# Values of the self attention in tiles of 128 tokens across batches, for the last three of four groups

## The chip, the cores and the metric

The kernel runs on one core of one Trainium2 chip. The metric is the device time of one execution in microseconds: the median of three runs, and beside it one execution that the hardware profiler recorded. An engine's name stands for its queue of instructions: TensorE (PE) for matrix products, VectorE (DVE), ScalarE (ACT) and GpSimd (POOL) for elementwise work, SyncE (SP) for issuing most of the DMAs. Each works through its queue in order.

## The reference, cut to what matters

One decoder layer on 16 batches of 100 tokens with 512 features: causal self attention with 16 heads of 32, cross attention to 361 context tokens per batch, a mixture of 8 experts, each followed by a residual sum and a norm. The change lies in the self attention:

```python
q = (x @ w_q.T).reshape(b, s, NH, HD).transpose(0, 2, 1, 3)
k = (x @ w_k.T).reshape(b, s, NH, HD).transpose(0, 2, 1, 3)
v = (x @ w_v.T).reshape(b, s, NH, HD).transpose(0, 2, 1, 3)
score = jnp.einsum('bhqd,bhkd->bhqk', q, k) * scale
...
attn = jax.nn.softmax(score, axis=-1)
o = jnp.einsum('bhqk,bhkd->bhqd', attn, v)
return o.transpose(0, 2, 1, 3).reshape(b, s, H) @ w_o.T
```

The values `v` are computed for each token by itself; batches meet nowhere in them. The output is float32.

## The kernel before, in words

**Splitting.** A float32 product is made of three products of reduced-precision float32 parts (`mm3`, L143): high by high, high by low, low by high, on lines L145, L146, L147. A contraction over 512 features has four chunks of 128, so one product of a tile (`mmk`) is 12 matmuls. `split` (L133) makes the parts: a cast for the high part (L137 on ACT, or L139), a subtraction for the low part (L140, on DVE or POOL).

**The first stage** (self attention, the first 207 us of the span) treats the batches in four groups of four (`GB` = 4, `GT` = 400 tokens). Each group has four units, one for each 128 features, that is four heads. In unit (g, c) the kernel computes:

- `self_q` and `self_k`: features by tokens, with the 400 tokens of the group as the moving operand (names pq, pk);
- `self_v` (L301): for each batch, tokens by features. The batch's 100 tokens are the stationary operand, so the result's partitions are tokens, and the 512 features move. The result (pv) is copied by ACT (L309) to a tile `v` of 100 partitions;
- `self_scores` (L326): products of queries and keys for each head and batch; `self_softmax` (L352) works on DVE, POOL and ACT;
- `self_turn` (L388): transposes the probabilities on PE (pt), copied by ACT to pT (L395);
- `self_attend` (L397): for each batch r and head, `V[g, r]` is the stationary operand, with tokens as the contraction, so the 100 tokens of a batch have to lie in partitions 0 to 99 of a tile of their own. The result is stored to DRAM (o1d, L416).

**Order.** The loop at L548 goes over the 16 units; `at(u, j, ...)` hangs further work ahead of turn j of unit u: the next unit's queries and keys, the fetch and split of the next group's tokens (`fetch_x`, `split_x`), the next group's values, and the rows of weights for the next stage (`fetch_row`, `split_row`; stored in slots of two large arrays WH and WL; they pass through a pool `stage` with three buffers). The compiler's scheduler then orders each engine's instructions within the dependences, by its own model, so the list of `at` is not the final order.

**The handover to the next stage** begins inside the first one. The output projection works on tiles of 128 tokens across batches: `b_fetch(t)` (L428) loads tile t of the attention output from DRAM (ol) and the residual (xr), `b_split` casts it (olp), `b_out` (L445) multiplies by the output weights (pa), adds and normalizes (L451, then `layernorm`), and stores (L453); `b_xT` (L455) transposes the result (ptx). Tiles 0 to 4 are projected before the last unit ends. `b_open` (L424) closes the pool `a_x`, which holds the incoming tokens xf, and opens a pool in its place for ol, xr and olp; `ol` has two buffers, `xr` four. The numbers in the list at L530 are 4 u + j: the first fetch hangs on 44, that is unit 11, turn 0.

After the first stage come the queries of the cross attention (`b_q`, pq at L600), the cross attention, the experts, and a last stage in which tile after tile is projected (pp), summed, multiplied by the norm's weight (L1529) and normalized (L1589, L1594, L1618), with square roots on ACT (L1653, q_f) and their refinement on DVE (L1654 to L1668).

Of the kernel before, what the change touches and what calls it, by code (L numbers as in the profile page):

```python
# [9 lines left out]
FP = mybir.dt.float32  # L10
# [7 lines left out]
B, S, D = 16, 100, 512  # L18
T = B * S
KC = D // 128  # L20
# [8 lines left out]
GB = 4  # L29
NG = B // GB  # L30
GT = GB * S
TT = [(t, min(128, T - t)) for t in range(0, T, 128)]
EPS_LN = 1e-5
EPS_RMS = 1e-6
# [28 lines left out]
def tile_decoder_layer(  # L63
    ctx: ExitStack,
    tc: tile.TileContext,
    x: bass.AP,
    xT: bass.AP,
    ctxT: bass.AP,
    mask: bass.AP,
    wqT: bass.AP,  # L70
# [21 lines left out]
    nc = tc.nc  # L92
# [3 lines left out]
    def pool(stack, name, bufs=1, **k):  # L96
        return stack.enter_context(
            tc.tile_pool(name=name, bufs=bufs, reuse_waits="tile", **k)
        )
# [6 lines left out]
    def bank(tag, shape, name):  # L106
        return ps[-1].tile(shape, FP, name=name, tag=tag)
# [12 lines left out]
    def in_turn(ins, prev):  # L120

        if prev is not None:
            tc.add_manual_dep(
                ins.ins,
                prev.ins.name,
                mybir.DependencyInfo(
                    mybir.DependencyClass.NoSync, mybir.DependencyReason.DATA
                ),
                reason="in_turn",
            )  # L130
        return ins

    def split(dst, src, high=None, low=None):  # L133

        high, low = high or nc.scalar, low or nc.vector
        if high is nc.scalar:
            ins = nc.scalar.copy(dst.h, src)  # L137
        else:
            ins = high.tensor_copy(dst.h, src)  # L139
        low.tensor_tensor(dst.l, src, dst.h.bitcast(FP), ALU.subtract)  # L140
        return ins

    def mm3(out, a, b, start, stop):  # L143

        nc.tensor.matmul(out, a.h, b.h, start=start, stop=False)  # L145
        nc.tensor.matmul(out, a.h, b.l, start=False, stop=False)  # L146
        nc.tensor.matmul(out, a.l, b.h, start=False, stop=stop)  # L147

    def mmk(out, a, b, n=KC):
        for k in range(n):  # L150
            mm3(out, a(k), b(k), k == 0, k == n - 1)
# [38 lines left out]
    stage = pool(ctx, "stage", 3)  # L190
# [5 lines left out]
    def slot_of(s):  # L196
        return Pair(WH[:, s], WL[:, s])
# [8 lines left out]
    units = {}  # L206
# [7 lines left out]

    NT = len(TT)
    o1d = [dram.tile([128, KC, GT], FP, name=f"o1d_{g}") for g in range(NG)]
    x1d = [dram.tile([128, D], FP, name=f"x1d_{t}") for t in range(NT)]
# [4 lines left out]
    a_l, a_r = ExitStack(), ExitStack()  # L222
    xp = pool(a_r, "a_x", 1, side="right")
    w1 = pool(a_l, "a_1", 1)
    w2 = pool(a_l, "a_2", 2)
    w3 = pool(a_l, "a_3", 8)
    ps.append(pool(a_l, "ps_a", 2, space=PSUM))
    ps_s = pool(a_l, "ps_s", 1, space=PSUM)

    xg, V, Q, K, O, P = {}, {}, {}, {}, {}, {}  # L230

    def fetch_x(g):
        xg[g] = xp.tile([128, KC, GT], FP, name=f"xf_{g}", tag="xf")
        nc.sync.dma_start(xg[g], xT[g])

    def x_pair(g):

        s = 6 + g % 2
        return Pair(WH[:, s, :, :GT], WL[:, s, :, :GT])

# [7 lines left out]
    XF = {}  # L248
    xf = xp.tile([128, KC, GT], FP, name="xf_0", tag="xf")
    xg[0] = x_pair(0)  # L250
# [46 lines left out]
    def split_chunk(c):  # L297
        split(*chunk("q", c), nc.scalar, nc.gpsimd)
        split(*chunk("k", c), nc.scalar, nc.gpsimd)

    def self_v(g, r):  # L301
        pv = bank("mm" if g else "t", [S, D], f"pv_{g}_{r}")
        mmk(
            pv,
            lambda k: xg[g][:, k, r * S : (r + 1) * S],
            lambda k: units["wv_s"][:, k, :],
        )
        V[g, r] = w1.tile([S, D], FP, name=f"v_{g}_{r}", tag="v", bufs=8)
        nc.scalar.copy(V[g, r], pv)  # L309

    def self_q(g, c):
        cc = slice(c * 128, (c + 1) * 128)
        pq = bank("mm", [128, GT], f"pq_{g}_{c}")
        mmk(pq, lambda k: units["wq_s"][:, k, cc], lambda k: xg[g][:, k, :])

        Q[g, c] = w2.tile([128, GT], FP, name=f"qT_{g}_{c}", tag="qT")
        nc.scalar.activation(Q[g, c], pq, AF.Copy, scale=-1.0 / math.sqrt(HD1))
# [79 lines left out]
    def self_attend(g, c):  # L397

        av = bank("t", [128, GB, S], f"av_{g}_{c}")
        prev = None  # L400

        for r in range(GB):
            for j in (3, 0, 1, 2):
                h = c * 128 + 32 * j
                ins = nc.tensor.matmul(
                    av[32 * j : 32 * j + 32, r, :],
                    V[g, r][:, h : h + 32],
                    PT[g, c, j][:, r, :],
                    start=True,
                    stop=True,  # L410
                    tile_position=(0, 32 * j),
                )
                prev = in_turn(ins, prev)
        o = w2.tile([128, GT], FP, name=f"o_{g}_{c}", tag="o")
        nc.scalar.copy(o, av.rearrange("p r s -> p (r s)"))
        nc.sync.dma_start(o1d[g][:, c], o)  # L416
# [11 lines left out]
    def b_fetch(t):  # L428
        t0, n = TT[t]
        OL[t] = ol = inp["b"].tile([128, KC, 128], FP, name=f"ol_{t}", tag="ol")  # L430
        a = t0
        while a < t0 + n:
            g, o = divmod(a, GT)
            m = min(GT - o, t0 + n - a)
            nc.sync.dma_start(ol[:, :, a - t0 : a - t0 + m], o1d[g][:, :, o : o + m])
            a += m
        XR[t] = inp["b"].tile([128, D], FP, name=f"xr_{t}", tag="xr", bufs=4)
        nc.sync.dma_start(XR[t][:n], x_flat[t0 : t0 + n, :])

    def b_split(t):  # L440
        n = TT[t][1]
        ol = OL[t]
        OL[t] = pair(inp["b"], [128, KC, 128], f"olp_{t}", tag="olp")
        return split(OL[t][:, :, :n], ol[:, :, :n], low=nc.gpsimd)

    def b_out(t):
        t0, n = TT[t]
        o, xr = OL.pop(t), XR[t]
        pa = bank("mm", [128, D], f"pa_{t}")
        mmk(pa[:n], lambda k: o[:, k, :n], lambda k: units["wo_s"][:, k, :])  # L450
        nc.vector.tensor_tensor(xr[:n], pa[:n], xr[:n], ALU.add)  # L451
        layernorm(xr[:n], xr[:n], n, f"ln1_{t}")
        nc.sync.dma_start(x1d[t][:n], xr[:n])  # L453

    def b_xT(t):  # L455
        t0, n = TT[t]
        x1 = XR.pop(t)
        pt = bank("t", [128, KC, 128], f"ptx_{t}")
        for k in range(KC):
            nc.tensor.transpose(  # L460
                pt[:, k, :n], x1[:n, k * 128 : (k + 1) * 128], ident[:n, :n]
            )
        X1T[t] = slot_of(0)[:, t % KC].rearrange("p (k n) -> p k n", n=128)
        split(X1T[t][:, :, :n], pt[:, :, :n])
# [3 lines left out]
    def at(u, j, f, *a):  # L468
        extra.setdefault((u, j), []).append(lambda: f(*a))
# [24 lines left out]
    for u, (g, c) in enumerate(heads4):  # L494
        if u + 2 < NU:
            if u < 2:
                at(u, 0, split_chunk, u + 2)
            at(u, 0, self_k, *heads4[u + 2])
            at(u, 2, self_q, *heads4[u + 2])
        if g + 1 < NG:  # L500
            if c == 0:
                at(u, 1, fetch_x, g + 1)
                for k in range(2):
                    at(u, 3, split_x, g + 1, k)
            if c == 1:
                for k in range(2):
                    at(u, 1, split_x, g + 1, 2 + k)
            if c > 1:
                for r in range(2):
                    at(u, 1 + 2 * r, self_v, g + 1, 2 * (c - 2) + r)  # L510

    rows = [("wo_s", 3, kp(woT), k) for k in range(KC)]
    rows += [("wq_0", 4, Wqg[0], k) for k in range(KC)]
# [8 lines left out]
    for k in range(KC):  # L522
        i = 4 * NU - 8 + k
# [2 lines left out]
        at(i // 4, i % 4, behind, split_row, "wq_3", k)  # L526

    AHEAD = 5
    at(10, 0, b_open)
    for t, i in enumerate((44, 48, 52, 54, 58)):  # L530
        at(i // 4, i % 4, b_fetch, t)
        i += 2 if t == AHEAD - 1 else 4
        at(i // 4, i % 4, behind, b_split, t)
    for t, i in enumerate((51, 55, 59, 61, 62)):
        at(i // 4, i % 4, b_out, t)
    for t, i in enumerate((57, 60, 63)):
        at(i // 4, i % 4, b_xT, t)
# [1 line left out]
    self_q(0, 0)  # L539
    self_k(0, 0)  # L540
    self_scores(*heads4[0])
    self_v(0, 0)
    split_chunk(1)
    for r in range(1, GB):
        self_v(0, r)
    self_q(0, 1)
    self_k(0, 1)
    for u, unit in enumerate(heads4):  # L548
# [15 lines left out]
    w1 = pool(b_l, "b_1", 1)  # L564
# [27 lines left out]
    def b_q(t):  # L592
        t0, n = TT[t]
        x1T = X1T.pop(t)
# [83 lines left out]
    w1 = pool(c_l, "c_1", 1, side="right")  # L678
# [183 lines left out]
    for i, (b, g) in enumerate(order):  # L862
# [34 lines left out]
        if i % 3 == 2 and 8 <= i < 8 + 3 * NKV * KC:  # L897
            w, k = divmod((i - 8) // 3, KC)
# [12 lines left out]
    w1 = pool(d_l, "d_1", 1, side="right")  # L911
# [416 lines left out]
    for i in range(HEAD * NKV, len(parts)):  # L1328
        t, g = parts[i]
# [477 lines left out]
```

## Time and profile before

| what | value |
|---|---|
| median of three runs | 1411.22 us (1411.13 to 1414.11) |
| the profiled execution, its own time | 1423.84 us |
| span of that execution | 1422.1 us |
| mean granted clock of PE in it | 0.973 |
| matmuls and their weight loads | 7952 each |
| DVE, ACT, POOL busy | 66%, 53%, 50% of the span |
| matmuls for values (pv) in the first stage | 192, in 16 products |
| copies of values, ACT L309 | 16, median 587 ns |
| weights rows fetched by SP in the first stage | 20 (4 for f_wo_s, 16 for f_wq) |

The span is what the profiler recorded between the first and the last instruction of one execution. That execution's own time is 0.9% above the median of the plain runs; its parts are used for differences. "Busy" of PE overstates: matmuls are pipelined, and each one's recorded duration overlaps the next one's. What a matmul costs in a row of matmuls is the distance between two starts. A weight load (PEld) stands in its own row.

### The profile page before, as it was taken

To read this page: it belongs to the slowest core of one execution; us is meant where nothing else is said; L and a number is where in the kernel's file an instruction comes from. 1 tells how busy PE (TensorE), PEld (TensorE's weight loads), DVE (VectorE), ACT (ScalarE), POOL (GpSimd) and SP (SyncE) were. 2 spreads that over 40 slices of the span, in tenths; PEclk is the share of its full clock that TensorE was granted. 3 is DMA by queue.
4 is the path that set the end of the run, shared out by engine and by line. 5 is a ranking of instruction groups with operands and counts; after the bars stand their busy time and mean duration, and the time that the engine had idled before them with its cause. 6 is when DMAs were issued, how large, how long until landed. Compare 5 with 4: busy or idle time off the path is not lost.

```text
span 1422.1 us, 25158 instructions
## 1 busy us (share of the span) xinstructions
PE 1338.8 (94%) x7952; PEld 1109.5 (78%) x7952; DVE 939.8 (66%) x2960; ACT 756.9 (53%) x1899; POOL 708.8 (50%) x837
## 2 busy tenths in 40 slices
PE   8999989999999999999999999999999897899895
PEld 6888868888878887888888788878887675677773
DVE  5776577776467777767777667767653658654577
ACT  4666653444445666666565666656563233233356
POOL 6877663344245555555555545545454345431530
PEclk9999989999999999999999999999999999799997
DMA  5221254545442222233233213232536555667773
GB/s 158 72 93 51 73 158 115 130 91 111 101 93 77 53 60 69 70 77 76 69 70 82 70 43 70 70 70 54 132 84 198 170 167 164 189 207 232 247 254 125
DMA packets 197872, 159.79 MB, mean 112 GB/s; under 512 B 133322, under 2 KB 152878, under 8 KB 197742
## 3 DMA queue, kind: packets, MB, share of 16 engines
q1 hardware_dynamic: 187904, 137.83, 36.3%
q0 software_dynamic: 4576, 14.95, 3.5%
q10 hardware_dynamic: 5262, 5.41, 1.3%
q8 instruction: 65, 1.06, 0.3%
q14 instruction: 65, 0.53, 0.1%
HBM read 107.16 MB, written 50.99 MB: 111 GB/s over the span
## 4 chain that ended last, share of the span: by engine, by line
PE 69%; DVE 13%; DMA 8%; ACT 4%; issue 3%; POOL 1%; SPq 1%; ACTq 0%; DVEq 0%; POOLq 0%
PE pq L145 4%; PE pq L147 4%; PE pq L146 4%; PE pv L145 4%; PE pv L146 4%; PE pv L147 4%; PE ptp L767 3%; PE pk L145 3%; PE pk L147 3%; PE pk L146 3%; PE s L145 3%; PE s L147 3%; PE s L146 3%; PE av L146 2%; PE av L145 2%
## 5 line engine op out<-in xcount | busy, mean ns | idle before, releaser
L759 POOL TENSOR_SCALAR p<-p,sums 100x361 f32<-100x361 f32 x256 | 146.5, 577 | 100.2 <-DVE sums L758 89.2
L746 DVE CUSTOM_DVE_ANT_0 p<-s,nmask 100x361 f32<-100x361 f32 x256 | 132.9, 527 | 64.4 <-PE s L147 56.0
L757 ACT ACTIVATE p<-p,nm 100x361 f32<-100x361 f32 x256 | 153.2, 601 | 40.1 <-DVE nm L746 37.0
L140 DVE TENSOR_TENSOR pT_l<-ptp,pT_h 128x400 fp32r<-128x400 f32 (+1 forms) x192 | 107.4, 567 | 57.3 <-ACT pT_h L137 56.7
L145 PE MATMUL pq<-WH 128*128 128x512 f32 (+2 forms) x272 | 107.2, 394 | 5.7 <-DVE WH L139 5.7
L767 PE MATMUL ptp<-ident,p 100*128 100x100 f32 (+1 forms) x768 | 107.5, 252 | 0.0
L137 ACT CAST pT_h<-ptp 128x400 fp32r<-128x400 f32 (+1 forms) x192 | 91.2, 486 | 29.6 <-PE ptp L767 29.1
L767 PEld LDWEIGHTS ptp<-ident,p 100*128 100x128 f32 (+1 forms) x768 | 95.6, 152 | 13.4 <-POOL p L759 2.3
L140 POOL TENSOR_TENSOR cT_l<-cf,cT_h 128x512 fp32r<-128x512 f32 (+1 forms) x48 | 54.3, 1133 | 101.9 <-ACT cT_h L137 100.0
L146 PE MATMUL pq<-WL,WH 128*128 128x512 f32 (+2 forms) x272 | 104.6, 385 | 0.0
L147 PE MATMUL pq<-WH,WL 128*128 128x512 f32 (+2 forms) x272 | 104.5, 384 | 0.0
L147 PE MATMUL acc<-WH,ot_l 128*128 128x512 f32 (+1 forms) x208 | 85.9, 414 | 7.4 <-DVE ot_l L140 5.6
L145 PE MATMUL acc<-WH,ot_h 128*128 128x512 f32 (+1 forms) x208 | 85.8, 413 | 4.9 <-ACT ot_h L137 4.9
L145 PE MATMUL s<-kT_h,WH 128*100 128x362 f32 x256 | 88.2, 355 | 1.7 <-ACT kT_h L137 1.7
L145 PE MATMUL av<-pT_h,WH 128*128 128x400 f32 (+1 forms) x192 | 77.3, 402 | 11.5 <-ACT pT_h L137 11.2
L147 PE MATMUL s<-kT_h,WL 128*100 128x362 f32 x256 | 84.5, 330 | 0.0
L146 PE MATMUL acc<-WL,ot_h 128*128 128x512 f32 (+1 forms) x208 | 84.3, 405 | 0.0
L146 PE MATMUL s<-kT_l,WH 128*100 128x362 f32 x256 | 83.9, 328 | 0.0
L614 POOL TENSOR_TENSOR qs<-qs,r_q 128x512 f32<-128x512 f32 (+1 forms) x52 | 54.0, 1068 | 59.3 <-DVE r_q L169 48.9
L140 POOL TENSOR_TENSOR WL<-qf,WH 128x400 fp32r<-128x400 f32 x64 | 67.3, 1052 | 30.1 <-ACT WH L137 26.7
L145 PE MATMUL pv<-WH,cT_h 128*128 128x512 f32 (+1 forms) x192 | 79.6, 414 | 0.9 <-DVE WL L140 0.9
L145 PE MATMUL pk<-WH,cT_h 128*128 128x512 f32 (+1 forms) x192 | 77.6, 404 | 0.2
(336 smaller groups left out, 4007.0 us busy)
## 6 DMA issues: line engine op xcount, KB each, us to landing
qf<-qd SPq DMA_DIRECT2D x64, 200.0 KB
of<-od SPq DMA_DIRECT2D x48, 256.0 KB
cf<-in_ctxT SPq DMA_DIRECT2D x16, 722.0 KB
eb<-in_expert_b SPq DMA_DIRECT2D x32, 256.0 KB
ysd<-h SPq DMA_DIRECT2D x32, 256.0 KB
f_e<-in_expert_w SPq DMA_DIRECT2D x30, 256.0 KB
f_wq<-in_Wq SPq DMA_DIRECT2D x16, 256.0 KB
f_wo<-in_Wo SPq DMA_DIRECT2D x16, 256.0 KB
```

The costliest lines, as they stand in the source:

```text
L137: ins = nc.scalar.copy(dst.h, src)
L140: low.tensor_tensor(dst.l, src, dst.h.bitcast(FP), ALU.subtract)
L145: nc.tensor.matmul(out, a.h, b.h, start=start, stop=False)
L146: nc.tensor.matmul(out, a.h, b.l, start=False, stop=False)
L147: nc.tensor.matmul(out, a.l, b.h, start=False, stop=stop)
L614: nc.gpsimd.tensor_tensor(qr[:, hs, :], qr[:, hs, :], rs[:n, hs].unsqueeze(2).to_broadcast([n, GR, HD2]), ALU.mult,)
L746: nc.vector.tensor_tensor_reduce(out=p, in0=sc[:, :SE], in1=nmask, scale=1.0, scalar=BIG, op0=ALU.add, op1=ALU.min, accum_out=nm,)
L757: nc.scalar.activation(p, p, AF.Exp, bias=nm, scale=-1.0, accum_out=sh)
L759: nc.gpsimd.tensor_scalar(p, p, sh, 1.0, ALU.mult, ALU.mult)
L767: nc.tensor.transpose(pt[:n, h, :], probs[h][:, c0 : c0 + n], ident[:S, :S])
```

## The change

The first group's values stay as they were, batch by batch (`self_v_batch`), now in tiles of 128 partitions of which 100 are used. For the other three groups, the group's 400 tokens are cut into three tiles of 128 tokens, whatever batch they belong to, and a rest of 16 tokens. The three rests, 48 tokens, are gathered on the host into a further input `xlT`, fetched by `fetch_x_last`, split by `split_x_last` (high part on DVE, low part on POOL) and multiplied in one product (`self_v_last`). The attention still needs each batch's values in partitions from 0 on, so each tile's result is copied by ACT and then moved from partition to partition by DMAs on SP: six for a group, of 28, 72, 56, 44, 84 and 16 tokens. Tile 0 is copied straight to batch 0's tile, whose partitions 100 to 127 hold the first 28 tokens of batch 1 until they are moved.

Tiles 1 and 2 (`vt`) take buffers of the pool `a_x`, so that pool closes later: `b_open` goes from unit 10 to unit 12, the first two fetches for the output projection from 44 and 48 to 48 and 50, their splits from 48 and 52 to 50 and 54, and the first two projections from 51 and 55 to 53 and 56.

```diff
-    def self_v(g, r):
-        pv = bank("mm" if g else "t", [S, D], f"pv_{g}_{r}")
+    def self_v_batch(r):
+
+        pv = bank("t", [S, D], f"pv_0_{r}")
         mmk(
             pv,
-            lambda k: xg[g][:, k, r * S : (r + 1) * S],
+            lambda k: xg[0][:, k, r * S : (r + 1) * S],
             lambda k: units["wv_s"][:, k, :],
         )
-        V[g, r] = w1.tile([S, D], FP, name=f"v_{g}_{r}", tag="v", bufs=8)
-        nc.scalar.copy(V[g, r], pv)
+        V[0, r] = w1.tile([128, D], FP, name=f"v_0_{r}", tag="v", bufs=8)
+        nc.scalar.copy(V[0, r][:S], pv)
+
+    NL = (NG - 1) * REST_V
+
+    def fetch_x_last():
+        XF["l"] = stage.tile([128, D], FP, name="xl_f", tag="f")
+        nc.sync.dma_start(XF["l"][:, : KC * NL], xlT.rearrange("p k n -> p (k n)"))
+
+    def split_x_last():
+        xg["l"] = slot_of(5)[:, 0, : KC * NL].rearrange("p (k n) -> p k n", n=NL)
+        f = XF["l"][:, : KC * NL].rearrange("p (k n) -> p k n", n=NL)
+        split(xg["l"], f, nc.vector, nc.gpsimd)
+
+    def self_v_last():
+
+        pv = bank("mm", [NL, D], "pv_last")
+        mmk(pv, lambda k: xg["l"][:, k, :], lambda k: units["wv_s"][:, k, :])
+        V["l"] = w4.tile([NL, D], FP, name="v_last")
+        nc.scalar.copy(V["l"], pv)
+
+    def self_v(g, t):
+
+        pv = bank("mm", [128, D], f"pv_{g}_{t}")
+        mmk(
+            pv,
+            lambda k: xg[g][:, k, t * 128 : (t + 1) * 128],
+            lambda k: units["wv_s"][:, k, :],
+        )
+        for r in range(GB) if t == 0 else ():
+            V[g, r] = w1.tile([128, D], FP, name=f"v_{g}_{r}", tag="v", bufs=8)
+        if t == 0:
+            vt = V[g, 0]
+        else:
+            vt = xp.tile([128, D], FP, name=f"vt_{g}_{t}", tag="f", bufs=2)
+        nc.scalar.copy(vt, pv)
+        a = S if t == 0 else t * 128
+        while a < (t + 1) * 128:
+            r, o = divmod(a, S)
+            m = min(S - o, (t + 1) * 128 - a)
+            nc.sync.dma_start(V[g, r][o : o + m], vt[a - t * 128 : a - t * 128 + m])
+            a += m
+        if t == 2:
+            a = (g - 1) * REST_V
+            nc.sync.dma_start(V[g, GB - 1][S - REST_V : S], V["l"][a : a + REST_V])
...
-                    V[g, r][:, h : h + 32],
+                    V[g, r][:S, h : h + 32],
...
-            if c > 1:
-                for r in range(2):
-                    at(u, 1 + 2 * r, self_v, g + 1, 2 * (c - 2) + r)
+            if c == 2:
+                at(u, 1, self_v, g + 1, 0)
+                at(u, 3, self_v, g + 1, 1)
+            if c == 3:
+                at(u, 1, self_v, g + 1, 2)
+    at(2, 1, fetch_x_last)
+    at(2, 3, split_x_last)
+    at(3, 0, self_v_last)
...
-    at(10, 0, b_open)
-    for t, i in enumerate((44, 48, 52, 54, 58)):
+    at(12, 0, b_open)
+    for t, i in enumerate((48, 50, 52, 54, 58)):
         at(i // 4, i % 4, b_fetch, t)
-        i += 2 if t == AHEAD - 1 else 4
+        i += 2 if t in (0, AHEAD - 1) else 4
         at(i // 4, i % 4, behind, b_split, t)
-    for t, i in enumerate((51, 55, 59, 61, 62)):
+    for t, i in enumerate((53, 56, 59, 61, 62)):
         at(i // 4, i % 4, b_out, t)
```

More of the change, by code (lines that the diff above doesn't have):

```diff
@@ L31 @@
 GT = GB * S
+REST_V = GT % 128
 TT = [(t, min(128, T - t)) for t in range(0, T, 128)]
@@ L67, in tile_decoder_layer @@
     xT: bass.AP,
+    xlT: bass.AP,
     ctxT: bass.AP,
@@ L226, in tile_decoder_layer @@
     w3 = pool(a_l, "a_3", 8)
+    w4 = pool(a_l, "a_4", 1)
     ps.append(pool(a_l, "ps_a", 2, space=PSUM))
@@ L541, in tile_decoder_layer @@
     self_scores(*heads4[0])
-    self_v(0, 0)
+    self_v_batch(0)
     split_chunk(1)
     for r in range(1, GB):
-        self_v(0, r)
+        self_v_batch(r)
     self_q(0, 1)
@@ L1768 @@
         "xT": x.reshape(NG, GT, KC, 128).transpose(0, 3, 2, 1),
+        "xlT": x.reshape(NG, GT, KC, 128)[1:, GT - REST_V :]
+        .transpose(3, 2, 0, 1)
+        .reshape(128, KC, (NG - 1) * REST_V),
         "ctxT": np.asarray(ctx_2048).reshape(B, SE, KC, 128).transpose(0, 3, 2, 1),
```

## The prediction

> **What bounds the kernel now.** I read the page's busy shares first, then the busy times of three stretches around the first stage's end (columns: length, busy time and count of each engine, granted clock of PE, DMA share, GB/s):
>
> ```profile
> PE 1338.8 (94%) x7952; PEld 1109.5 (78%) x7952; DVE 939.8 (66%) x2960; ACT 756.9 (53%) x1899; POOL 708.8 (50%) x837
> ```
>
> ```profile
> 0.00:188.00 188.00, 181.19 (x1808) 152.74 (x1808) 120.18 (x281) 113.33 (x320) 135.62 (x153) 1.00 0.28 88
> 188.00:207.00 19.00, 13.77 (x123) 10.85 (x121) 15.52 (x34) 11.87 (x28) 15.87 (x15) 0.82 0.57 171
> 207.00:212.00 5.00, 5.00 (x19) 3.99 (x16) 0.95 (x4) 0.49 (x1) 0.08 (x1) 0.66 0.89 237
> ```
>
> PE bounds the first stage up to 188 us; then comes a handover of 19 us in which it has holes and a slower clock. The waits of PE between 36 and 212 us (waiter, releaser, total us, times, longest) confirm that the holes lie in the handover alone: the first stage has no wait above 0.2 us before it.
>
> ```profile
> PE pt L393 <- ACT pT L395: 3.8, 2, 2.4
> PE av L405 <- ACT pT L395: 1.4, 2, 0.8
> ```
>
> Third, the timeline of a value product, and of an output projection, which has the shape that the change gives the values (128 stationary columns, 512 moving):
>
> ```profile
> 99.76 0.39 PE L147 MATMUL pv<-WH,WL 128*100 128x512 f32 x1
> 99.77 0.16 PEld L145 LDWEIGHTS pv<-WH 128*100 128x100 f32 x1
> 99.99 0.39 PE L145 MATMUL pv<-WH 128*100 128x512 f32 x1
> 99.99 0.16 PEld L146 LDWEIGHTS pv<-WL,WH 128*100 128x100 f32 x1
> 100.22 0.40 PE L146 MATMUL pv<-WL,WH 128*100 128x512 f32 x1
> ...
> 179.42 0.40 PE L146 MATMUL pa<-WL,olp_h 128*128 128x512 f32 x1
> 179.43 0.19 PEld L147 LDWEIGHTS pa<-WH,olp_l 128*128 128x128 f32 x1
> 179.66 0.39 PE L147 MATMUL pa<-WH,olp_l 128*128 128x512 f32 x1
> ```
>
> The recorded 0.39 us is not the price. Starts are: from 99.53 to 101.84 ten steps of a value product, 0.231 us each; from 178.72 to 181.06 ten steps of a projection, 0.234 us each. The 512 moving columns set it; the stationary ones hardly count. That is why 100-token tiles waste time.
>
> **The change, part by part.**
>
> *Matmuls removed.* Twelve products of three groups become nine plus one: 24 matmuls fewer. 24 x 0.231 = 5.5 us. Each product also has a slow first step (99.21 to 99.53, 0.32 instead of 0.231): two fewer, 0.2 us. The 108 matmuls that now have 128 stationary columns pay 0.003 more, 0.3 us. Net **5.4 us**, all on the path, since PE has no waits there.
>
> [...] If the load stood between matmuls, the 108 would pay 0.024 each, 2.6 us, and the gain would be 5.7 - 2.6 = 3.1. But in the timeline each load begins together with the previous matmul, in the same rows, and is over before the next one starts; from 100 to 128 columns the step grows by 0.003, not by 0.024. The trace decides: 5.4, with 3.1 as the far end.
>
> *Moves between partitions.* 18 DMAs on SP, and the fetch of `xlT`. An issue of a similar size, o1d<-o, takes 0.33 us: 19 x 0.33 = 6.3 us of SP's time within 207, and SP mostly waits. No row has a transfer from partition to partition; the nearest, the fetch ol<-o1d (256 KB) in the chain of waits, takes 3.49 us to land; these move 32 to 168 KB. Bounds: nothing, or the whole latency on the path. After the last tile's product: ACT copy 0.59, two issues 0.7, landing 3.5: 4.8 us. By the order in which the built kernel puts PE's instructions, between group 1's last value product and its first use stand two q and two k products (each 12 x 0.18 = 2.2), four sets of transposes (0.35 each), two sets of scores (0.9) and one attention (0.8): 12.8 us; groups 2 and 3 have more. So I cost it at nothing; with the cover gone it would be up to 3 x 4.8 = 14 us.
>
> *What queues behind them.* The moves wait on SP for ACT's copies, and rows of weights stand behind. The tightest, the third output row, is issued once the 48-token tile is copied, and its cast stands 12 places further on ACT; ACT runs 70 instructions in the 36 us from 72 on, so 12 places are 6.2 us against 0.4 + 3.5. Covered. ACT itself has two copies less (1.2 us), DVE and POOL one small split more (128x192; the 128x400 one on POOL takes 1.05): off the path.
>
> *The handover.* Its rows now:
>
> ```profile
> 188.19 1.66 POOL L363 TENSOR_TENSOR p<-p,nm 100x400 f32<-100x400 f32 x2 [3.95 <-PE pt L393]
> ...
> 190.53 0.91 PE L393 MATMUL pt<-ident,p 100*100 100x100 f32 x4 [2.38 <-ACT pT L395]
> ...
> 199.52 1.88 SPq L435 DMA_DIRECT2D ol<-o1d  x3
> ...
> 203.69 0.62 ACT L137 CAST olp_h<-ol 128x512 fp32r<-128x512 f32 x1 [1.55 <-DMA ol<-o1d]
> ...
> 206.15 0.90 PE L405 MATMUL av<-pT,v 100*32 100x100 f32 x32 [0.85 <-ACT pT L395]
> ...
> 206.98 0.50 PE L145 MATMUL pq<-WH 128*128 128x512 f32 x1
> ```
>
> From the end of tile 2's projection (187.2) to the next stage's first product (206.98) are 19.8 us. PE's work in it, at the undisturbed steps: 24 pa x 0.234, 7 sets of transposes x 0.35, 3 ptx x 0.45, 2 attentions x 0.82 = 11.1. So 8.7 are lost, partly to the slow clock. Two waits stand out. PE waits 2.38 at 188.15: the last unit's exponentials stand on ACT ahead of the copy that frees the transposes' bank, and they wait for POOL, which got its input at 188. And ACT waits 1.55 for tile 6, its cast standing ahead of the last two copies of turned probabilities.
>
> In the built order, the projections of tiles 1 and 2 (22 matmuls, 5.1 us) now stand between the last scores and these transposes, so the softmax has time: the 2.38 go. Tile 6's cast moves behind one more of the copies, though its fetch also goes behind one more residual fetch: the 1.55 go. Against that, tile 5's fetch waits for POOL's low part of tile 3, now behind all four normalizations of the last unit instead of behind one (0.83 each, so 2.5 later): of these I take 1.5 to be uncovered at ACT's cast, an estimate. Sum -2.38 - 1.55 + 1.5 = **-2.4**. The ends: -6 if most of the loss goes, and +4 if the later `b_open` and both new orders cost another gap like the worst two together (2.38 + 1.55). I take the sum of the rows.
>
> *The end of the kernel.* The diff doesn't touch it, but the scheduler's order does: on DVE and ACT the last 40 or so instructions are permuted; everything between, on PE from the second stage on, is in the same order. The last rows now:
>
> ```profile
> 1411.65 0.68 DVE L1523 TENSOR_TENSOR z<-pp,z 64x512 f32<-64x512 f32 x1
> ...
> 1413.34 0.20 ACT L1653 ACTIVATE q_f<-sq 128x2 f32<-128x2 f32 x1 [0.21 <-DVE sq L1545]
> 1413.53 1.52 ACT L1618 ACTIVATE y<-y,m,r_f 128x512 f32<-128x512 f32 x2
> ...
> 1417.79 0.81 ACT L1618 ACTIVATE y<-y,m,r_f 64x512 f32<-64x512 f32 x1 [1.25 <-DVE m L1617]
> ```
>
> The last tile's sum (0.6) and weighting (0.7) move ahead of tile 11's residual step: +1.3. The two outputs at 1413.53 move ahead of the root at 1413.34; they used to cover the 1.4 us from that root to the last tile's variance, which now follow them: +1.4. Tile 12's square (0.58 and its accumulator 0.1) leaves the path: -0.7. Sum **+2.0**, ends 0 and +3.5.
>
> Total: -5.4 - 2.4 + 2.0 = **-5.8 us**. The profiled execution would go from 1423.84 to 1418.0; the plain runs lie 12.6 below it, and I carry the difference over as it is: 1411.2 - 5.8 = **1405.4**.
>
> **Rivals.**
>
> 1. *The handover improves much* (waits and slow clock nearly gone): -5.4 - 6 + 1 = -10.4, **1400.8**. For it: 8.7 us are lost there. Against: the tail of the last unit (transposes, copies, attention) is a chain through ACT, which no order removes.
> 2. *The handover gains nothing*: -5.4 + 2.0 = -3.4, **1407.8**; with the far end of the end-order about 1409. For it: a wait that goes usually uncovers the next, here tile 5's or tile 6's cast.
> 3. *Slower: ACT stalls on fetched tiles in the handover.* Tiles 0 and 1 are fetched at 86 us now; afterwards not before the pool closes behind the last move of values, near 140. With two `ol` buffers every later fetch waits for the split of two tiles earlier, and each cast stands in ACT's queue ahead of copies that PE waits for. If three of the five casts come one landing late (3 x 3.5) the handover grows by 10 less the 2.4 gained: -5.4 + 8 + 2 = +4.6, **1415.8**. It decides from +6.2 in the handover on (2.8 + 5.4 - 2.0). Against it: in the built order the first tile's cast comes many ACT instructions after its fetch.
> 4. *The moves are late*: one landing of 4.8 at each of three groups, +14 - 5.8 = +8, **1419**. Against: 12.8 us of cover. The change does what it says in any case: the built kernel has the 24 matmuls fewer.
>
> **How the numbers follow.** This kernel's measurement can't tell apart less than about 0.2% (2.8 us). Chances: forecast 0.48, first rival 0.12, second 0.22, third 0.13, fourth 0.05. Faster: 0.46 of the forecast, 0.12, and 0.10 of the second: 0.68. Slower: the third and fourth, less a little that stays within the bound: 0.16. Same: 0.16. Range: low end 1400.5 (first rival), high end 1412.5 (matmul gain 3.1, handover unchanged, end +3.5, that is +0.4, and something of the third rival); about 2 in 10 stay outside.
>
> **What would show it.** 168 matmuls named pv, 0.23 us apart; PE without waits for DMA at the attention products (a wait of av on v shows rival 4). The stretch from tile 2's projection to the first pq of the second stage: 17.4 instead of 19.8. No wait of 2.4 at the transposes; a wait of ACT at tile 5's cast. Waits of ACT for ol of several us show rival 3. From PE's last matmul (start 1409.32) to the last output step (1417.79), 8.5 now, some 10.5 after.

## The result, and the profile after

The changed kernel took 1408.02 us (median of 20 runs, 1403.33 to 1412.27), the kernel before in the same session 1411.18 us (20 runs): a ratio of 0.9975, 95% interval 0.9963 to 0.9987, which is 3.5 us less (1.8 to 5.2; the two medians themselves differ by 3.2). A second session gave 0.9980 (0.9967 to 0.9994). The gain is small but clear of the noise, and about six tenths of the forecast 5.8.

The profiled execution after has a span of 1410.1 us. Busy shares first, then the busy times of three stretches (columns as before), cut at the last step of tile 2's projection and at the first product of the second stage:

```profile
PE 1333.2 (95%) x7928; PEld 1107.4 (79%) x7928; DVE 945.2 (67%) x2961; ACT 757.0 (54%) x1897; POOL 711.2 (50%) x838
```

```profile
0.00:181.50 181.50, 175.14 (x1776) 149.69 (x1776) 122.65 (x276) 112.62 (x318) 137.90 (x157) 1.00 0.31 100
181.50:203.00 21.50, 14.84 (x130) 11.11 (x128) 18.60 (x42) 11.59 (x29) 14.17 (x13) 0.87 0.57 180
203.00:208.00 5.00, 5.00 (x16) 3.95 (x13) 0.16 (x1) 0.49 (x1) 0.00 (x0) 0.52 0.81 239
```

There are 24 matmuls fewer, and the last step of tile 2's projection starts 5.3 us earlier than before (186.75). But the handover that followed lasted 20.2 us before and lasts 21.6 now, with the same 129 matmuls from that step on, and VectorE is busy in 18.6 of the 21.5 us of the middle row. The waits of PE between 36 and 212 us show that the holes were moved, not removed (waiter, releaser, total us, times, longest):

```profile
PE av L452 <- ACT y_ln L160: 2.9, 1, 2.9
PE pt L440 <- DVE WL L142: 1.4, 1, 1.4
PE pt L440 <- ACT pT L442: 1.3, 2, 1.1
PE ptx L507 <- ACT pT L442: 0.9, 1, 0.9
```

The wait of 2.38 us at the transposes is not gone, it is split. The same set of transposes now waits 1.08 us and the next set 1.44, together 2.5, and a wait of 2.9 stands at the last unit's attention, where it was 0.85. Two instructions of VectorE, both named `t_ln`, stand behind these waits. The first comes before the handover (rows of three timelines):

```profile
175.22 2.43 DVE L163 SCALAR_TENSOR_TENSOR t_ln<-y_ln,v_ln 128x1 f32<-128x1 f32 x1
...
178.65 0.38 ACT L417 ACTIVATE p<-p,nm 100x100 f32<-100x100 f32 x1 [2.95 <-DVE nm L408]
...
183.86 0.55 PE L440 MATMUL pt<-ident,p 100*100 100x100 f32 x4 [1.08 <-ACT pT L442]
185.85 0.55 PE L440 MATMUL pt<-ident,p 100*100 100x100 f32 x4 [1.44 <-DVE WL L142]
```

The last unit's row minima (nm) stand behind it on VectorE, so ScalarE waits 2.95 us for them before that unit's exponentials, and copies of turned probabilities stand behind these. The second `t_ln` is in the chain of waits through the handover (start, length, what was waited for or ran):

```profile
186.61 3.62 DVE t_ln L163
...
190.65 0.55 DVE xr L183
...
191.52 0.02 SPq L500
...
200.22 0.60 ACT olp_h L139
...
201.01 0.38 ACT pT L442
...
201.52 1.56 PE av L452 x32
```

`t_ln` is one step of Newton's method for the layer norm's inverse root, on one number per partition; in the group of five its shortest takes 0.2 us. Here it runs 3.6. The store of tile 1's normalized rows (SPq L500) waits for it, and SP works through its queue behind that store almost without a gap, up to the fetch of tile 6 (ol):

```profile
191.22 0.32 SPq L500 DMA_DIRECT2D x1d<-xr  x1
191.59 1.40 SPq L527 DMA_DIRECT2D f_wq<-in_Wq  x3
193.03 0.43 SPq L500 DMA_DIRECT2D x1d<-xr  x1
193.50 1.09 SPq L463 DMA_DIRECT2D o1d<-o  x1
194.71 0.44 SPq L485 DMA_DIRECT2D xr<-in_x  x1
195.24 2.27 SPq L482 DMA_DIRECT2D ol<-o1d  x3
```

The second part of tile 6's fetch is issued at 195.82 and has landed at 200.11; ScalarE casts the tile at 200.21, and behind the cast come the last copy of turned probabilities and the attention. The chain view names another releaser for this cast, GpSimd's third split of a weight row. But by the times in the trace the cast starts at 200.209 and that split ends at 200.212, so the cast did not wait for it.

What runs beside this `t_ln` is seen in the timelines of GpSimd and of VectorE at that moment:

```profile
186.47 1.29 POOL L142 TENSOR_TENSOR olp_l<-ol,olp_h 128x512 fp32r<-128x512 f32 x1
187.72 1.27 POOL L142 TENSOR_TENSOR WL<-f_wq,WH 128x512 fp32r<-128x512 f32 x1
188.94 1.27 POOL L142 TENSOR_TENSOR olp_l<-ol,olp_h 128x512 fp32r<-128x512 f32 x1
```

```profile
186.53 3.70 DVE L163 SCALAR_TENSOR_TENSOR t_ln<-y_ln,v_ln 128x1 f32<-128x1 f32 x1
```

VectorE's instruction starts 0.06 us after the first of GpSimd's three subtractions and ends with the third (190.23 and 190.21). Such an instruction is called **held** below; that GpSimd holds it is read from the matching ends. The rows name two tensors as inputs of each of these instructions. The `t_ln` at 175.22 ends in the same way, at 177.65, with GpSimd's second subtraction beside it (177.63).

Two other answers of the trace. The moves, as issues on SP, and from issue to landing:

```profile
L352 SPq DMA_DIRECT2D v<-vt x12: 765/792/814, 58.4 to 152.6; - x12
L352 SPq DMA_DIRECT2D v<-v x3: 799/811/985, 54.7 to 137.7; - x3
L356 SPq DMA_DIRECT2D v<-v_last x3: 560/563/611, 66.3 to 144.2; - x3
...
DMA to landing us min/median/max: 2.0/2.2/3.0
```

And the kernel's end: the two full outputs now stand ahead of the root, as forecast.

```profile
1400.20 1.52 ACT L1670 ACTIVATE y<-y,m,r_f 128x512 f32<-128x512 f32 x2
1401.62 0.19 ACT L1705 ACTIVATE q_f<-sq 128x2 f32<-128x2 f32 x1
```

### The profile page after: what moved, and what is told of

The parts are those of the page before. It is cut to its first block, busy times and chain, and to the rows that moved or that the text cites. A ratio compares the mean times of both kernels' runs of the same rounds, so it can differ in the third digit from the quotient of the medians.

```text
span 1410.1 us, 25163 instructions
## 1 busy us (share of the span) xinstructions
PE 1333.2 (95%) x7928; PEld 1107.4 (79%) x7928; DVE 945.2 (67%) x2961; ACT 757.0 (54%) x1897; POOL 711.2 (50%) x838
## 4 chain that ended last, share of the span: by engine, by line
PE 70%; DVE 15%; DMA 6%; ACT 4%; issue 3%; POOL 1%; SPq 1%; ACTq 0%; DVEq 0%; POOLq 0%
PE pq L147 4%; PE pq L148 4%; PE pq L149 4%; PE pv L147 4%; PE pv L148 4%; PE pv L149 4%; PE ptp L819 3%; PE pk L147 3%; PE pk L149 3%; PE pk L148 3%; PE s L147 3%; PE s L148 3%; PE s L149 3%; PE av L148 2%; PE av L147 2%
## 5 line engine op out<-in xcount | busy, mean ns | idle before, releaser
L148 PE MATMUL pv<-WL,cT_h 128*128 128x512 f32 (+1 forms) x192 | 77.7, 405 | 0.0
```

## The experiments

The measure is the **stretch**: from the start of the last step of tile 2's projection to the first pq of the second stage.

**1 and 2. Both kernels again, unedited**, for the scatter between executions.

> The changed kernel once more, unedited: a second profile, which shows how far the times of a stage vary from one execution to the next. Theory (the handover's new order costs what it was to bring, since VectorE's two-input instruction t_ln is held by GpSimd): the end of tile 2's projection within 0.5 us of 181.7, the first product of the second stage within 0.5 us of 203.0, so 21.3 us between them, and t_ln again held for over 2 us near 186. Rival (the 21.3 us of the first profile is an accident of one execution): the stretch differs by over 1.5 us. The further 8 us by which the two first profiles part after the second stage has begun should not come back if they are variation: the whole span may then differ by several us while the first 203 us repeat.

> The kernel before once more, unedited, for the same purpose. The end of tile 2's projection within 0.5 us of 187.2 and the first product of the second stage within 0.5 us of 207.0 (19.8 us between) if the stages up to there repeat; over 1.5 us away if the first profile was an accident. The span may differ by several us from 1422.

Changed: last step at 181.50, pq at 201.85, stretch 20.35 (first profile 181.45, 203.01, 21.56). Before: 186.37, 205.70, 19.33 (first 186.75, 206.98, 20.23). So up to tile 2 the stages repeat within 0.4 us, and the handover within about 1.2. The first two profiles part by 8 us more after the handover. That is within what executions of one program differ by: the spans of the changed kernel were 1410.1 and 1401.9, those of the kernel before 1422.1 and 1410.5. In the second profile of the changed kernel `t_ln` was held for 1.24 us at the same place, not for over 2 as expected, and the next instruction with two inputs for 1.18: each about as long as one of GpSimd's subtractions (1.27 to 1.29 in the first profile) instead of three.

**3. What 128 stationary columns cost.** In the kernel before:

```diff
-        pv = bank("mm" if g else "t", [S, D], f"pv_{g}_{r}")
+        m = 128 if g and r < GB - 1 else S
+        pv = bank("mm" if g else "t", [m, D], f"pv_{g}_{r}")
...
-            lambda k: xg[g][:, k, r * S : (r + 1) * S],
+            lambda k: xg[g][:, k, r * S : r * S + m],
...
-        nc.scalar.copy(V[g, r], pv)
+        nc.scalar.copy(V[g, r], pv[:S])
```

> The kernel before, but nine of its twelve value products of the last three groups load 128 stationary columns instead of 100; the 28 further rows are not used. Same count of matmuls, no moves, no later handover. This measures alone what a step with 128 columns costs against one with 100. Theory (the moving columns set the step, 0.231 against 0.234 us): the end of tile 2's projection 0.3 us later than in the kernel before, 187.5. Rival (the load stands between the matmuls, 0.024 us longer each): 108 x 0.024 = 2.6 us later, 189.8. The whole time: the same within 0.1% by the theory, 0.2% slower by the rival.

The last step of tile 2's projection came at 186.95, against 186.37 and 186.75: 0.2 to 0.6 later, not 2.6. The timeline of one such product in this kernel:

```profile
63.66 0.40 PE L145 MATMUL pv<-WH 128*128 128x512 f32 x1
63.90 0.40 PE L146 MATMUL pv<-WL,WH 128*128 128x512 f32 x1
64.13 0.40 PE L147 MATMUL pv<-WH,WL 128*128 128x512 f32 x1
```

The mean of 84 undisturbed steps with 128 columns is 0.2329 us, of 30 with 100 columns in the same kernel 0.2310. The ratio of the times is 0.9996 (0.9979 to 1.0014). The longer loads cost 0.002 us a step and not 0.024; the rival falls.

**4. The later handover list alone**, in the kernel before:

```diff
-    at(10, 0, b_open)
-    for t, i in enumerate((44, 48, 52, 54, 58)):
+    at(12, 0, b_open)
+    for t, i in enumerate((48, 50, 52, 54, 58)):
...
-        i += 2 if t == AHEAD - 1 else 4
+        i += 2 if t in (0, AHEAD - 1) else 4
...
-    for t, i in enumerate((51, 55, 59, 61, 62)):
+    for t, i in enumerate((53, 56, 59, 61, 62)):
```

> The kernel before, with its values untouched, and only the changed kernel's list for the handover: the pool of the next step opens two units later, tiles 0 and 1 of the heads' outputs are fetched at places 48 and 50 instead of 44 and 48, the second of their splits two places earlier, projections of tiles 0 and 1 at 53 and 56 instead of 51 and 55. Theory (the later list makes the handover longer, since the low parts of the splits and GpSimd's softmax products now stand back to back and hold VectorE): the stretch from tile 2's projection to the first product of the second stage grows from 19.8 to about 21.3 us, and t_ln is held for over 3 us in it. Rival (the list by itself costs nothing, and the 1.5 us come from the moves and the order in which the changed values leave ScalarE and SyncE): the stretch stays within 0.7 us of 19.8. Rival in the other direction (the list brings the 2.4 us that were forecast, and the moves take them back): the stretch falls to about 17.4.

The last step comes at 186.53 and pq at 208.94: a stretch of 22.41, and a ratio of 1.0025 (1.0007 to 1.0043), slightly slower. No single `t_ln` was held for the 3 us that were expected; the longest took 2.54. The chain of waits of this kernel runs through the Newton steps:

```profile
192.79 2.03 DVE t_ln L161
...
195.03 0.59 DVE r_ln L169
195.62 2.46 DVE t_ln L161
...
198.68 0.64 PE ptx L460 x4
```

Three operations on one column take 5.1 us of the path; PE's transposes of the normalized tile wait 2.24 us for them.

**5 and 6. A Newton step that reads one tensor**, in the changed kernel, profiled and timed in two sessions, the second with the unedited kernel beside it:

```diff
-            nc.vector.scalar_tensor_tensor(
-                t[:p], y[:p], y[:p], v, ALU.mult, ALU.mult
-            )
+            nc.vector.tensor_scalar(t[:p], y[:p], y[:p], v, ALU.mult, ALU.mult)
...
-        nc.vector.tensor_tensor(r[:p], t[:p], y[:p], ALU.mult)
+        if n == 1:
+            nc.vector.tensor_scalar(r[:p], t[:p], y[:p], None, ALU.mult)
+        else:
+            nc.vector.tensor_tensor(r[:p], t[:p], y[:p], ALU.mult)
```

> The changed kernel, in which the Newton step of the layer norm's inverse root reads one tensor from SBUF instead of two: t_ln and r_ln of one column are made by TENSOR_SCALAR, with the second factor as the scalar per partition. Same values, same count of instructions on VectorE. TENSOR_SCALAR on 128x1 never took over 0.16 us in any trace so far, while t_ln took up to 3.70. Theory (VectorE held in these two instructions by GpSimd's two-input products lengthens the handover): no operation on 128x1 over 0.5 us, and the stretch from tile 2's projection to the second stage's first product falls from 20.4 to 21.6 us (counted from the start of the last pa step, as in the two profiles of the changed kernel) to about 19.4; the median time about 1.5 us below that of the changed kernel. Rival (the holding is real but beside the path; ScalarE's queue, with casts that wait for fetched tiles, sets the handover): the holding goes and the stretch stays at 20.4 to 21.6.

> The changed kernel with the one-input Newton step, once more. Theory (being held by GpSimd is what took the forecast gain of the handover): the first product of the second stage within 1 us of 198.8 and the stretch near 17.2 again, 3 to 4 us below the unedited changed kernel, and a median 2 to 4 us below it (a ratio near 0.995 against the kernel before). Rival (the first profile was a lucky execution): the stretch is back at 20 or above.

> The changed kernel, unedited, timed in the same call as the version with the one-input Newton step, so that both ratios are against the same runs of the kernel before. All theories: a ratio near 0.9975. Its profile is a third look at the stretch from the last step of tile 2's projection to the second stage's first product: 20.4 to 21.6 us, with t_ln held for over 1 us at about 186.5.

The stretch is 17.20 and 17.16 (pq at 198.81 and 198.67); unedited it is 21.42 (202.92), with `t_ln` held for 3.70 again. Ratios to the kernel before 0.9956 (0.9938 to 0.9973) and 0.9973 (0.9959 to 0.9986), the unedited one 0.9980 in the second session. The scheduler kept the handover's order but for neighbours: on ScalarE the last turned copy goes ahead of one operation of 0.2 us, on PE two matmuls of a projection go ahead of one set of transposes, on VectorE a few operations move by one place, on SP one fetch by one. The groups of `t_ln` between 36 and 212 us, unedited (first) and edited (second; busy us, mean ns):

```profile
L163 DVE SCALAR_TENSOR_TENSOR t_ln<-y_ln,v_ln 128x1 f32<-128x1 f32 x5 | 8.0, 1600 | 2.4 <-ACT y_ln L160 2.4
```

```profile
L163 DVE TENSOR_SCALAR t_ln<-y_ln,v_ln 128x1 f32<-128x1 f32 x5 | 1.4, 271 | 2.2 <-ACT y_ln L160 2.1
```

Both held places gain. The last unit's exponentials start 2.0 us earlier:

```profile
176.65 0.38 ACT L418 ACTIVATE p<-p,nm 100x100 f32<-100x100 f32 x1 [0.78 <-DVE nm L409]
183.51 0.95 PE L441 MATMUL pt<-ident,p 100*100 100x100 f32 x8 [0.72 <-ACT pT L443]
```

The two sets of transposes wait 0.72 us together, where it was 2.5. The fetch of tile 6 lands at 196.16 instead of 200.11. PE's waits of over 0.15 us in the stretch sum to 3.9 and 3.8 us, against 6.6, 4.7 and 6.5 in the three unedited profiles. The rest of the gain goes with the clock: PE's granted clock was one half for 2.3 and 2.6 us of the stretch, against 5.4, 6.8 and 4.8.

What ends last in the edited kernel is again the fetch of tile 6, by its chain of waits, and the row behind shows how the second stage begins:

```profile
186.42 4.81 DMA x1d<-xr
...
191.30 0.66 SPq L486
...
192.00 4.16 DMA ol<-o1d
...
196.26 0.62 ACT olp_h L139
196.88 0.40 ACT pT L443
...
197.32 1.56 PE av L453 x32
```

```profile
198.80:203.00 4.20, 4.20 (x14) 3.32 (x11) 0.13 (x1) 0.49 (x1) 0.00 (x0) 0.50 0.69 202
```

The residual's buffer waits for a store to land, the second part of the fetch of ol stands behind it on SP, and the cast behind that. Then the second stage begins at a granted clock of 0.50: 14 products in 4.2 us, which at 0.23 us would take 3.2.

The whole time shows less than the stretch, and less than the 2 to 4 us expected: in the shared session the medians differ by 1.0 us (1413.96 and 1412.97, 22 runs each). At the second stage's last pq the gain is about 2.9 (389.1 and 388.9 against 393.5, 390.1 and 392.1). In the last stage the executions of one kernel differ by far more: from the first to the last product pp 76.1 and 85.5 us in the edited kernel's two profiles. Where the rest of the 2.9 goes can't be told from these.

**7. The same edit in the kernel before.**

> The same edit of the Newton step in the kernel before. There t_ln was held for 2.69 and 1.34 us (2.33 and 1.34 in the second profile) at times when PE's waits named ScalarE's copies. Theory: if holding matters there as much, the stretch (20.2 and 19.3 from the start of the last pa step) falls by about 1 us too, to 18.8; then the holding is no part of what the change did. If it matters only with the changed list, it stays at 19.3 to 20.2.

The last step comes at 186.21 and pq at 205.54: a stretch of 19.33, as in the second profile of the unedited kernel. One run took 1412.57 us. Yet the holding was on the path here too. The chain of waits of the kernel before, in its first profile, has the wait for tile 6 that the prediction lists, and a held `t_ln` at its start:

```profile
194.94 2.70 DVE t_ln L161
...
198.63 0.33 SPq L453
...
200.10 3.49 DMA ol<-o1d
...
203.69 0.62 ACT olp_h L137
```

Without the holding another chain ends as late: from 194 to 202 us it is PE's own work, at first 0.43 us apart instead of 0.23.

**8. The old list in the changed kernel**: the diff of experiment 4 backwards, and the last group's two `vt` tiles in the weights' staging pool, since they would otherwise need the pool that this list closes:

```diff
-            vt = xp.tile([128, D], FP, name=f"vt_{g}_{t}", tag="f", bufs=2)
+            vp, k = (stage, {}) if g == NG - 1 else (xp, {"bufs": 2})
+            vt = vp.tile([128, D], FP, name=f"vt_{g}_{t}", tag="f", **k)
```

> The changed kernel with the handover's list of the kernel before: the pool of the next step opens at unit 10 again, fetches of tiles 0 and 1 at places 44 and 48, projections of tiles 0 and 1 at 51 and 55, the second split two places later. The two value tiles of the last group that would still need the closed pool go through buffers of the weight staging pool. Theory (the list lengthens the handover; the matmuls saved are as forecast): the end of tile 2's projection stays near 181.7, and the stretch after it, from the start of the last pa step, is 19.3 to 20.2 as in the kernel before instead of 20.4 to 21.6: the first product of the second stage at about 201.3, 1 us earlier. Rival (the 1.2 us come from the moves or from ScalarE's shorter lead, whatever the list): the stretch stays at 20.4 to 21.6. Rival (the forecast's reason was right and the old list keeps the wait of 2.4 us at the transposes): the wait returns.

This is a miss for the theory. The stretch is 19.9 as it says, but tile 2's projection ends later (last step at 183.74), since PE waits 1.5 for VectorE's reciprocals at 173.6, 0.5 for a turned copy at 179.5 and 0.2 for a low part at 181.5; pq comes at 203.62, not at 201.3. The first set of transposes waits 2.33 and the next 0.60, 2.9 together against 2.5 with the later list: the wait is in one piece again, as the second rival says, but the later list had hardly shortened it. Ratio 0.9971 (0.9954 to 0.9989), no different from the later list's.

**9, 10 and 11. Both edits together**, in each kernel, the one of the kernel before also timed.

> The kernel before with the later handover list and the one-input Newton step. With the list alone the first product of the second stage came at 208.94, against 205.7 to 207.0 in the kernel before, and t_ln was held three times, for 2.02, 2.54 and 1.23 us. Theory (the later list costs time by putting GpSimd's two-input products beside the Newton steps): the first product comes 2 to 3 us earlier, at about 206.5. Rival (the later list costs by its order alone): it stays at 208.5 to 209.4.

> The changed kernel with the old handover list and the one-input Newton step. With the old list alone the first product of the second stage came at 203.62, and only one t_ln was held, for 1.09 us. Theory (what the later list brings shows only where VectorE isn't held): the edit gains under 1 us here, 202.7 to 203.6, so that the later list with the edit, 198.8, is the better of the four. Rival (the edit shortens the handover under any list): about 200.

> The kernel before with the later handover list and the one-input Newton step, its values untouched, timed. Its first profile put the first product of the second stage at 201.66, 1.3 us before the changed kernel, though it does 24 matmuls more: a handover of 15.1 us from the start of the last step of tile 2's projection. Theory (list and edit together bring about 4 to 5 us, whatever the values do): 201.7 within 1 us again and a ratio near 0.997 against the kernel before, about what the changed kernel has. Rival (the first profile was a lucky execution): the first product at 204 or later, and a ratio within 0.001 of 1.

The kernel before with the later list and the one-input step has pq at 201.66 and 202.49, stretches 15.1 and 15.8, where the list alone had 22.4. The edit gains about 7 us there, more than twice what was expected. PE's waits in the stretch fall from 6.7 to 2.6 and 3.1 us, and PE's clock, at one half for 6.8 us of the stretch with the list alone, stays at 1.00 throughout. Ratio 0.9977 (0.9968 to 0.9986): as much as the changed kernel has, without touching the values. Its order on PE, ScalarE and GpSimd is that of experiment 4 throughout the first stage, so the difference is VectorE's, but for one fetch of a residual that moves by one place on SP. The changed kernel with the old list and the edit has its last step at 181.68, pq at 202.28 and a stretch of 20.6. The edit doesn't shorten the stretch, but it brings tile 2's projection forward by 2.1 us and pq by 1.3, where under 1 was expected. This pair is no clean test: the order of PE, ScalarE and VectorE differs in several places between the two, and the clock stood at one half for 7.2 us of the stretch instead of 3.4. In one run it took 1419.18 us.

All stretches together, in us:

| values | list | two inputs | one input |
|---|---|---|---|
| as before | old | 20.2, 19.3 | 19.3 |
| as before | later | 22.4 | 15.1, 15.8 |
| changed | old | 19.9 | 20.6 |
| changed | later | 21.6, 20.4, 21.4 | 17.2, 17.2 |

Read by rows: the edit shortens the stretch clearly only with the later list. Read by columns: with the one-input step the later list is better than the old one by 3.4 to 4.2 us; with the two-input step it is worse by 0.5 to 3.1. Four of the eight boxes are single profiles, and one program's profiles differ by up to 1.2 us.

## Why the prediction was right, and where not

The measured 1408.0 us lies in the range that was given, 2.6 above the forecast 1405.4. By the parts below, the handover missed by 3.7 us, and the end of the kernel, forecast 1.1 too long, gave some of that back by luck.

- **Matmuls, -5.4: right.** The last step of tile 2's projection comes at 181.48 (mean of three profiles) instead of 186.56 (of two), 5.1 less. All 168 matmuls are in the record (156 named pv, 12 pv_last). Steps with 128 columns are 0.2305 apart in the changed kernel. The far end of 3.1 supposed that the loads stand between the matmuls, so that the difference of their lengths (means 0.164 us for 100 columns, 0.188 for 128) is paid at each step. No run shows this loss: in the changed kernel the load at 56.95 takes 0.19 us beside the matmul of 0.39 that starts with it, and the next matmul starts at 57.17. Experiment 3 has 0.002 us a step instead of 0.024, so 3.1 falls as an end.
- **Moves, nothing: right, with a wrong size.** An issue takes 0.56 to 0.81 us, not 0.33, so SP spends 12 x 0.79 + 3 x 0.81 + 3 x 0.56 = 13.6 us on the moves instead of 6.3 for all. They land in 2.0 to 3.0 us, under the 3.5 taken. The last moves of group 1 are issued from 69.79 on over 1.67 us and so are there by 74.5; its first attention is at 82.87. No attention product waits for a DMA. The fourth rival falls.
- **Handover, -2.4: this step failed.** It became +1.3 (21.1, mean of three, against 19.8, mean of two). The step took two waits as gone because the order of PE and ScalarE changes, and it put at nothing that a `t_ln` on VectorE can be held. The 2.38 at the transposes became 1.08 and 1.44, behind a `t_ln` held for 2.43 us; the 1.55 at tile 6's cast became 1.17, behind one held for 3.7 us by way of a store and SP's queue. At tile 5's cast, costed at 1.5 more, the wait was 0.64, for PE and not for its fetch. The last unit's attention waits 2.88 instead of 0.85. The trace before already had the sign: the chain to tile 6's wait of 1.55 starts at a `t_ln` held for 2.70. With the one-input step the stretch is 17.2, 2.6 under the kernel before, close to the 2.4 forecast. That it fits so well is partly chance: tile 5's cast waits 3.9 us for its fetch in that version, and part of the gain is the clock, which the step did not sum.
- **End of the kernel, +2.0: right in sign, too large.** From the last product pp to the last output step: 8.5 and 8.7 before, 9.5, 9.5 and 9.3 after, +0.9. The outputs do stand ahead of the root as the step said; the three terms of its sum were not told apart. The end goes with each build's order and not with the values: among versions of the kernel before it is 9.5 in experiment 7 and 7.4 in experiments 3 and 4.
- **The sum.** -5.1 + 1.3 + 0.9 = -2.9, against 3.5 less measured (1.8 to 5.2) and 2.8 in the second session (0.9 to 4.7). The second rival's figure, 1407.8, was met. Its reason is confirmed in part: what ends last is tile 6's cast, which waits 1.17 us for its own fetch, but that fetch is late because of VectorE's Newton step. The third rival's mechanism, ScalarE standing at a cast for a fetched tile, is there too, with these 1.17 us and, in the version without holding, with 3.9 and 0.65; the "several us" that would have decided for it did not come in the changed kernel as it is.

What the failed step left out is seen in the runs. With two tensors as inputs `t_ln` took up to 3.70 us, as long as three of GpSimd's subtractions of 1.27 to 1.29 us one behind the other. With one tensor and factors per partition it took 0.27 us, also in the middle of GpSimd's products (at 180.18 in experiment 9, where these run for 2.70 us from 179.48 on). Why the two forms differ was not shown.

The version with the one-input step has the lowest ratios to the kernel before, 0.9956 and 0.9973. Its interval overlaps the unedited changed kernel's, so that it beats the kernel before is shown; that it beats the changed one is shown for the handover alone. Whether a third buffer for ol would take away the next wait wasn't tried.

## What to carry to other kernels

When a change moves GpSimd's work, look at what VectorE does at those moments: here a tiny instruction that reads two tensors stood for 3.7 us beside three GpSimd subtractions, and a DMA queue behind it turned that into a late fetch. For one value per partition, the product with the second factor as the scalar operand took 0.27 us at most in the first stage of the edited kernels. An edit and an order can each bring nothing alone and several us together, as in the first two rows of the table, so test them in pairs before dropping either.

## What was not expected of the hardware

The holding isn't the same in every execution: at the same place it lasted 3.70, 1.24 and 3.70 us in three profiles of one program. In the profile with 1.24, GpSimd paused for 0.13 us after its first subtraction, waiting for a cast, and VectorE's instruction ended within 0.02 us of that subtraction's end; in the other two profiles the three subtractions ran without a pause. A pause is not needed: at 196.78 in the first profile `t_ln` was held for 0.99 us and went on at the boundary between two subtractions. What decides it stays open.

The clock that PE gets after a thin stretch was not expected either. With 3.9 to 4.0 us of PE work in the 6.5 from 181.5 on, the granted clock between 188 and 191.5 us was 0.61, 0.50 and 0.53 in these three profiles, with products up to 0.43 us apart instead of 0.23. In the two profiles with the one-input step PE had 5.5 us of work in the same 6.5, and the clock between 188 and 191.5 was 1.00. So in these runs the lower clock came with the larger holes and added to what they cost. Whether the holes bring it, and how thin the work must be for it, was not measured.
